# First block of a two-layer transformer kernel: the second group's rows loaded ahead of the FFN weights, bias and FFN statistics by tiles, FFN rows normalised on ScalarE, softmax sums ahead of the pieces' additions

## Chip, core and metric

The kernel runs on one core of one Trainium2 chip. The metric is the device time of one execution in microseconds (us). Three timed runs of the kernel before gave 2656.91, 2652.33 and 2652.30; the median is 2652.33. Engines are written as in the profile: PE is TensorE (matmuls), PEld its weight loads, DVE VectorE, ACT ScalarE, POOL GpSimd, SP SyncE, from whose queue all DMAs are issued. All data are float32.

## What is computed

The reference takes x of 2 sequences x 2048 tokens x 256 features through four sublayers; only the first is touched by the change. Cut to it:

```python
x = L0_attn_x                                   # (2, 2048, 256)
x = x + _L0_attn_ref(_layernorm(x), ...)        # first block
# within _L0_attn_ref(x, ...):
h = _layernorm(x, g1, b1)
q, k, v = h @ Wq + bq, h @ Wk + bk, h @ Wv + bv # 16 heads of 16, 4 key heads
q, k = _rope(q), _rope(k)
scores = q k^T / 4, masked to a window of 64    # each token sees itself and 63 before it
out = softmax(scores) @ v
x = x + (out @ Wo + bo)
h2 = _layernorm(x, g2, b2)
return x + gelu(h2 @ Wf1 + bf1) @ Wf2 + bf2     # FFN, 1024 wide
```

After it come a local attention block with an FFN (two layers), a gated block over the whole sequence, and a product with ternary weights.

## The kernel before

The 4096 tokens are 32 tiles of 128 (a tile: tokens on the 128 partitions), in 8 groups of four. The first block works tile by tile in steps. The table `steps` (lines 635 to 661) says which stage of which tile or group stands in which step: tile t is projected and taken (rope) in step t, its scores, masks and maxima stand in step t + 1, its transposed weights and values in t + 2, its output projection in t + 3. The first seven tiles (RAMP = 7) are projected a step early, as no FFN work fills their steps. For group g the first-layernorm statistics stand in step 4g - 3, its normalisation and transposes in 4g - 2, together with the residual rows y (`residual`, line 307), and the bias bo is added to y in step 4g + 1, four tiles at once. When a group's last tile is done, in step s = 4g + 7, the FFN of the group begins: `FfnA.statistics` over its four tiles and `FfnA.normalise`; its eight hidden products and four output products ("pieces") fill the next four steps in two places each, fill(0) and fill(1), and in step s + 5 the finished rows get their statistics and go, normalised, into R for the next block.

Inside a step, `step_a` (line 666) writes out the order by hand. PE, ACT, DVE and POOL each run their instructions strictly in that order (`manual_schedule`, line 1446); only the DMA queue of SP is ordered by the compiler's own scheduler. So what stands first in the text holds up whatever stands behind it on the same engine. Semaphores order the engines among each other.

Lines that the prediction speaks of:

- DMA: line 56 issues every load. Line 318 to 347 load the weights; the group's rows are loaded by `GroupA.__init__` (line 294), the values of a tile are copied to a shifted place by lines 431 and 433 (`vown` to `vmid`), and FFN weights of the next block are loaded in the step that projects tile 4 (line 673).
- First layernorm: L145 and L146 (DVE, statistics of one tile), L158, L159, L162 (POOL, power -1/2), L169 (rows normalised on DVE) or L176 and L178 (the same on ACT), L224 (PE transposes of a group), L229 (ACT takes them with gain and shift), L188 and L193 (residual rows y on ACT), L216 (POOL, four row additions, of the bias and of others).
- Tile: L402 (PE projection), L411, L425 (DVE), L417, L420, L428 (POOL), L438, L443 (DVE), L449, L450 (PE transposes), L455, L456, L458 (ACT copies), L468 (PE scores), L478 (DVE masks), L487 (DVE maxima), L488 (POOL subtracts them), L491 (ACT exponents), L522 (PE transposes of weights), L530 (ACT copies), L542 and L550 (PE values and sums), L560, L561 (DVE), L566 (PE output), L572 (DVE adds it to y). From tile 6 on the sums of the weights come from DVE instead of PE: L498 (sums), L501 (reciprocal), L508 (ACT spreads), L513 (PE transposes), L515 (ACT copies).
- FFN: L604 (PE hidden), L610 (ACT gelu), L615 (PE output), L622 (DVE addition), L135, L137 (POOL, power), L207 (rows normalised on DVE), L625 (stores the finished rows).
- Next block, in the change of block: L973 (PE projection), L985 (ACT), L994, L997 (POOL), L1029 (PE transposes), L1048 (PE scores).

The region allocator (`Region`, line 93) places the tiles of this block by tag in one large buffer, `room`; a tag with one buffer is written again only when its last reader is through.

Of the kernel before, what the change touches and what calls it, by code (L numbers as in the profile page):

```python
# [17 lines left out]
P = 128  # L18
# [27 lines left out]
def kernel(ctx: ExitStack, tc: tile.TileContext, I: dict, out: bass.AP):  # L46
# [241 lines left out]
    class GroupA:  # L288


        def __init__(self, g):
            self.g = g
            self.xg = T(wa, [P, GT, D], "xg", 1)
            load(self.xg, x_v[:, g * GT : (g + 1) * GT, :])
# [15 lines left out]

        def add_bias(self):
            add_rows(self.y, lambda t: boA)

# [15 lines left out]
    ropeA = T(wA, [P, TPS, 2, AHD], "ropeA")  # L329
    load(ropeA, I["rope_a"])  # L330

    woA = T(wA, [P, KC, D], "woA")
# [56 lines left out]
    class TileA:  # L389
# [94 lines left out]
        def maxima(self, half):  # L484
            Sh = self.S[:, half * 2 * AG : (half + 1) * 2 * AG, :]
            mc = T(small, [P, 2 * AG], "mxA")
            nc.vector.reduce_max(mc, Sh, axis=AX.X)  # L487
            nc.gpsimd.tensor_sub(Sh, Sh, mc.unsqueeze(2).to_broadcast([P, 2 * AG, P]))  # L488

        def exponents(self):  # L490
            nc.scalar.activation(self.S, self.S, AF.Exp, scale=1.0 / AHD**0.5)  # L491

# [81 lines left out]
    class FfnA:  # L574


        def __init__(self, grp):
            self.g, self.y = grp.g, grp.y
            self.xr = T(wa, [P, GT, D], f"xr{self.g % 2}", 1)
            load(self.xr, x_v[:, self.g * GT : (self.g + 1) * GT, :])  # L580

        def statistics(self):
            self.stats = statistics(self.y)

        def normalise(self):
            self.h = T(wa, [P, GT, D], "h", 1)
            if self.g == 0:
                mv, rs = self.stats
                normalised_on_scalar(self.y, mv[:, :, 0], rs, self.h)
            else:  # L590
                normalised(self.y, self.stats, self.h)
            add_rows(self.y, lambda t: bf2)

            add_rows(self.xr, lambda t: self.y[:, t, :])
# [28 lines left out]

        def last_statistics(self):
            nc.sync.dma_start(out=xs[:, self.g * GT : (self.g + 1) * GT, :], in_=self.xr)  # L625
            self.stats = statistics(self.xr)

# [19 lines left out]
    for g in range(NG):  # L647
        at(GT * g - 5, "load", g)
        at(GT * g - 3, "statistics", g)
        at(GT * g - 2, "normalise", g)  # L650
        at(GT * g + 1, "bias", g)
        s = GT * (g + 1) + 3
        at(s - 1, "residual", g)
        at(s, "prepare", g)

        if g < NG - 1:
            for c in range(ADFF // P):
                at(s + 1 + c // 4, f"fill{c // 2 % 2}", g, "hidden", c)
            for tt in range(GT):
                at(s + 3 + tt // 2, f"fill{tt % 2}", g, "output", tt)  # L660
        at(s + 5, "finish", g)

    groups_a, tiles_a, ffns_a = {0: first_group}, {}, {}
    steps_a = steps

    def step_a(todo):
        p = a = q = o = n = m = f = e = None
        for (g,) in todo.get("load", ()):
            if g:
                groups_a[g] = GroupA(g)  # L670
# [10 lines left out]
        if "output" in todo:  # L681
            o = tiles_a.pop(todo["output"][0][0])
        for (g,) in todo.get("residual", ()):
            ffns_a[g] = FfnA(groups_a[g])
        if "statistics" in todo:
            n = groups_a[todo["statistics"][0][0]]
        if "normalise" in todo:
            m = groups_a[todo["normalise"][0][0]]
        if "prepare" in todo:
            f = ffns_a[todo["prepare"][0][0]]  # L690
        if "finish" in todo:
# [15 lines left out]
        for (t,) in todo.get("project", ()):  # L707
            tiles_a[t].project()
        if p and p.t < RAMP:
            p.take()  # L710
            if q:
                q.mask(0)
                q.mask(1)
            p.rotate()
            if q:
                q.maxima(0)
                q.mask(2)
        else:
            if q:
                q.mask(0)  # L720
                q.mask(1)
            if p:
                p.take()
            if q:
                q.mask(2)
            if p:
                p.rotate()
            if q:
                q.maxima(0)
# [4 lines left out]
        if a and not pieces:  # L734
            a.weights_to_keys()
            a.take_weights()
        for r in pieces:
            r()
        if n:
            n.statistics()  # L740
        if f:
            f.statistics()
        if e:
            e.last_statistics()
        if o and not o.by_features:
            o.spread_sums()
        if p:
# [5 lines left out]
        if a and pieces:  # L753
            a.weights_to_keys()
            a.take_weights()
        for r in fill(1):
            r()
        if m:
            m.normalise()
        if f:  # L760
            f.normalise()
        if e:
# [10 lines left out]
        if m:  # L773
            m.to_features()
            m.residual()
        if f:
            f.to_features()
        if a and not a.by_features:
            a.sum_weights()
        for (g,) in todo.get("bias", ()):  # L780
            groups_a[g].add_bias()

# [1013 lines left out]
```

## Time and profile before

| what | us |
|---|---|
| median of three timed runs | 2652.33 |
| profiled execution, its own time | 2654.86 |
| its span, first to last instruction | 2653.1 |
| PE busy / DVE busy / ACT busy / POOL busy | 2569.6 / 1620.1 / 1221.2 / 993.9 |
| 0 to 15, PE busy and granted clock | 5.70 at 1.00 |
| 15 to 30 | 8.66 at 0.94 |
| 30 to 45 | 7.15 at 0.50 |
| 45 to 60 | 14.04 at 0.99 |
| 60 to 121 | 49.58 at 0.92 |
| 183 to 244 (one group of the steady part) | PE 59.00, DVE 50.46, ACT 36.20, POOL 34.96 |
| 491 to 552 (change to the next block) | 51.30 at 0.94 |

How to read it: the times in the profile are those of one execution, from its first instruction. A row of the timeline has the start, the duration, the engine, the line of the kernel, the operation, what it writes and reads, how many such instructions are merged, and in brackets how long the engine stood idle ahead of it and what ended that. Matmuls overlap, and their ends are modelled, so PE's busy time is no measure of its peak; holes between its rows are. The granted clock is the share of full speed at which TensorE was clocked.

### The profile page before, as it was taken

The numbers are of one execution on the slowest core, as the hardware profiler recorded it, in microseconds if no ns is written. First come the engines' busy times: TensorE is split into PE (matmuls) and PEld (weight loads), VectorE is DVE, ScalarE is ACT, GpSimd is POOL, SyncE is SP. The second block draws the span as 40 slices with busy tenths as digits, with TensorE's granted clock in tenths as the row PEclk, the third lists the DMA queues.
The fourth block names the chain that finished last, engine by engine and source line by source line (L and its number), as shares of the span: only waits on it lengthen the run. The fifth ranks groups of instructions, "written<-read, shape, count | busy, mean of one in ns | idle before, by whom it ended". The sixth has DMA issues, their size and how long they took to land.

```text
span 2653.1 us, 50755 instructions
## 1 busy us (share of the span) xinstructions
PE 2569.6 (97%) x19766; PEld 1638.2 (62%) x19766; DVE 1620.1 (61%) x4403; ACT 1221.2 (46%) x2567; POOL 993.9 (37%) x1237
## 2 busy tenths in 40 slices
PE   6899999898999999999999999999999999999998
PEld 4566666566667666666666676666544445445567
DVE  5778877557666776657666677774433435434344
ACT  3565655465666666656566666663510001500000
POOL 5555554445444444444544544541200002300011
PEclk8999999998999999999999999999999999999999
DMA  5010111111001101010311111101100000100000
GB/s 170 17 31 30 33 31 39 47 33 48 21 21 25 29 25 26 21 59 21 97 29 25 29 33 37 25 17 58 40 8 4 7 6 12 44 0 7 4 10 12
DMA packets 73167, 81.99 MB, mean 31 GB/s; under 512 B 18829, under 2 KB 57056, under 8 KB 72672
## 3 DMA queue, kind: packets, MB, share of 16 engines
q1 hardware_dynamic: 72928, 78.75, 10.7%
q8 instruction: 157, 2.57, 0.4%
q14 instruction: 82, 0.67, 0.1%
HBM read 44.20 MB, written 10.50 MB: 21 GB/s over the span
## 4 chain that ended last, share of the span: by engine, by line
PE 82%; DVE 9%; POOL 4%; issue 3%; DMA 1%; ACT 1%; SPq 1%; POOLq 0%; ACTq 0%; DVEq 0%
PE ps L1649 16%; PE ps L973 12%; PE ps L1227 10%; PE ps L1250 6%; PE ps L1573 4%; PE ps L1155 4%; PE ps L1048 3%; PE ps L1126 2%; PE ps L604 2%; PE ps L1592 2%; PE ps L1561 2%; PE ps L1098 2%; PE ps L1029 2%; PE ps L1551 2%; PE ps L615 2%
## 5 line engine op out<-in xcount | busy, mean ns | idle before, releaser
L1649 PE MATMUL ps<-room 128*128 128x512 f32 (+1 forms) x1152 | 463.2, 544 | 0.0
L1649 PEld LDWEIGHTS ps<-room 128*128 128x128 f32 x1152 | 217.8, 189 | 221.9 <-issue 214.7
L973 PE MATMUL ps<-room 128*128 128x512 f32 x768 | 347.2, 601 | 0.0
L1079 ACT ACTIVATE room<-room,shift,rn 128x192 f32<-128x192 f32 x512 | 276.0, 546 | 72.9 <-DVE shift L1067 72.9
L994 POOL TENSOR_TENSOR room<-room 128x256 f32<-128x256 f32 x128 | 112.9, 882 | 500.5 <-ACT room L985 500.5
L1227 PE MATMUL ps<-room 128*128 128x512 f32 x640 | 287.6, 593 | 0.4 <-ACT room L229 0.4
L1617 ACT COPY room<-ps 128x256 f32<-128x256 f32 x32 | 11.8, 370 | 587.9 <-PE ps L1615 587.9
L1012 POOL TENSOR_TENSOR rn<-ss,mhalf 128x8 f32<-128x8 f32 x128 | 248.5, 1941 | 10.7
L973 PEld LDWEIGHTS ps<-room 128*128 128x128 f32 x768 | 141.0, 190 | 157.7 <-issue 150.2
L1579 DVE SCALAR_TENSOR_TENSOR room<-ps,room 128x512 f32<-128x512 f32 (+1 forms) x144 | 90.1, 626 | 206.5 <-PE ps L1573 206.5
L1227 PEld LDWEIGHTS ps<-room 128*128 128x128 f32 x640 | 118.8, 190 | 137.3 <-issue 131.8
L1602 POOL TENSOR_SCALAR veC<-mvC 128x1 f32<-128x1 f32 x32 | 7.2, 224 | 453.1 <-DVE mvC L1600 453.1
L1250 PE MATMUL ps<-room 128*128 128x256 f32 x768 | 173.0, 379 | 0.0
L1060 DVE CUSTOM_DVE_ANT_0 room<-ps,room 128x192 f32<-128x192 f32 x512 | 152.2, 353 | 15.0 <-PE ps L1048 14.2
L1250 PEld LDWEIGHTS ps<-room 128*128 128x128 f32 x768 | 143.7, 190 | 24.8 <-issue 6.5
L1090 DVE TENSOR_SCALAR room<-room,rdB 128x192 f32<-128x192 f32 x512 | 151.7, 360 | 4.5
L1243 DVE SCALAR_TENSOR_TENSOR room<-ps,room 128x512 f32<-128x512 f32 x96 | 72.1, 751 | 125.8 <-PE ps L1227 87.0
L488 POOL TENSOR_TENSOR room<-room,mxA 128x1024 f32<-128x1024 f32 x64 | 120.3, 1896 | 58.8 <-DVE mxA L487 33.3
L1009 DVE TENSOR_REDUCE ss<-room 128x8 f32<-128x512 f32 x128 | 81.9, 681 | 94.3 <-ACT room L987 94.3
L1573 PE MATMUL ps<-room 128*128 128x512 f32 (+1 forms) x288 | 133.4, 545 | 0.0
L1155 PE MATMUL ps<-room 128*128 128x256 f32 x512 | 120.9, 379 | 0.0
L1155 PEld LDWEIGHTS ps<-room 128*128 128x128 f32 x512 | 97.3, 190 | 34.1 <-issue 23.2
(190 smaller groups left out, 5032.7 us busy)
## 6 DMA issues: line engine op xcount, KB each, us to landing
room<-room SPq DMA_DIRECT2D x144, 128.0 KB
room<-in_L_attn_x_dram SPq DMA_DIRECT2D x16, 512.0 KB
room<-in_rope_b_dram SPq DMA_DIRECT2D x16, 512.0 KB
xs<-room SPq DMA_DIRECT2D x8, 512.0 KB
room<-xs SPq DMA_DIRECT2D x8, 512.0 KB
room<-in_rope_c_dram SPq DMA_DIRECT2D x8, 512.0 KB
out_dram<-R SPq DMA_DIRECT2D x32, 128.0 KB
room<-in_L_ffn_w_dram SPq DMA_DIRECT2D x6, 640.0 KB
```

The lines of the kernel that those rows point to most:

```text
L488: nc.gpsimd.tensor_sub(Sh, Sh, mc.unsqueeze(2).to_broadcast([P, 2 * AG, P]))
L973: nc.tensor.matmul(pm, src[:, cols], self.w["wqkv"][:, k, part * BIN : (part + 1) * BIN], start=k == 0, stop=k == 1,)
L994: nc.gpsimd.tensor_mul(u2[:, :, 0:hd2], x[:, :, hd2:BHD], sin[:, :, 0:hd2].to_broadcast([P, BH, hd2]))
L1012: nc.gpsimd.tensor_tensor(self.rn[part], ss, mhalf[:, 0:BH], ALU.pow)
L1060: nc.vector.tensor_tensor_reduce(S[:, e, jj, :], sc[e][:, jj * KW : (jj + 1) * KW], self.mask[:, jj, :], 1.0, -3.0e38, ALU.add, ALU.max, t ...
L1079: nc.scalar.activation(S[:, e, jj, :], S[:, e, jj, :], AF.Exp, bias=self.shift[half][:, a : a + 1], scale=self.rn[0][:, head : head + 1], ...
L1090: nc.vector.tensor_scalar_mul(S[:, e, jj, :], S[:, e, jj, :], rd[:, a : a + 1])
L1155: nc.tensor.matmul(pm[:, 0:D], self.oT[:, k, :], wo[:, k, :], start=k == 0, stop=k == BIN // P - 1)
L1227: nc.tensor.matmul(pm, w["w1"][:, k, half, c * P : (c + 1) * P], hT[:, k, :], start=k == 0, stop=k == KC - 1,)
L1250: nc.tensor.matmul(pm[:, 0:D], hh[:, c, tt * P : (tt + 1) * P], self.w["w2"][:, c, :], start=c == 0, stop=c == BNC - 1,)
L1573: nc.tensor.matmul(pm[:, 0:n], self.KT[:, J * P : (J + 1) * P], self.QT[:, q0 : q0 + n], start=True, stop=True,)
L1649: nc.tensor.matmul(acc[e][:, 0:n], self.V[:, J, e * P : (e + 1) * P], s2, start=J == 0, stop=J == TPS - 1,)
```

## The change

- The second group's rows are loaded right behind the rope table, ahead of Wo and the FFN weights (`second_group = GroupA(1)`), into the place `xr1`, since `xg` holds the first group. Its statistics stand in step 0 instead of 1, its normalisation and transposes in step 1 instead of 2, its residual rows in step 3 instead of 2.
- The bias is added to y one tile a step (steps 4g + 1 to 4g + 4) instead of four tiles in step 4g + 1.
- The FFN's statistics are taken one tile a step, each after the tile's output is added; the last at the very start of step s. The finished rows' statistics are split in two steps of two tiles.
- The FFN rows are normalised on ACT in all groups (before: group 0 alone), right behind the copies of the weights (L530), and the additions on POOL follow where the whole stood before.
- The sums of the weights (L498, L501) stand ahead of the additions of fill(1), and their spreading (L508) ahead of fill(0)'s gelus or additions; before, both stood behind them.
- In the first seven tiles the exponents are two instructions of half a tile each.
- The maxima lie in the region (two buffers) instead of the small pool (three).

No arithmetic is added or left out.

```diff
-            self.xg = T(wa, [P, GT, D], "xg", 1)
+            self.xg = T(wa, [P, GT, D], "xr1" if g == 1 else "xg", 1)
...
-        def add_bias(self):
-            add_rows(self.y, lambda t: boA)
+        def add_bias(self, i):
+            nc.gpsimd.tensor_add(self.y[:, i, :], self.y[:, i, :], boA)
...
     load(ropeA, I["rope_a"])
+    second_group = GroupA(1)
...
-            mc = T(small, [P, 2 * AG], "mxA")
+            mc = T(wa, [P, 2 * AG], "mxA")
...
-            nc.scalar.activation(self.S, self.S, AF.Exp, scale=1.0 / AHD**0.5)
+            for S in (self.S[:, 0 : 2 * AG, :], self.S[:, 2 * AG :, :]) if self.t < RAMP else (self.S,):
+                nc.scalar.activation(S, S, AF.Exp, scale=1.0 / AHD**0.5)
...
-        def statistics(self):
-            self.stats = statistics(self.y)
+        def statistics(self, i):
+            st = T(small, [P, 6], "st")
+            nc.vector.bn_stats(st, self.y[:, i, :])
+            nc.vector.bn_aggr(self.mv[:, i, :], st)
+            if i == GT - 1:
+                self.rs = rstd_of(self.mv)
...
             self.h = T(wa, [P, GT, D], "h", 1)
-            if self.g == 0:
-                mv, rs = self.stats
-                normalised_on_scalar(self.y, mv[:, :, 0], rs, self.h)
-            else:
-                normalised(self.y, self.stats, self.h)
+            normalised_on_scalar(self.y, self.mv[:, :, 0], self.rs, self.h)
+
+        def residual(self):
             add_rows(self.y, lambda t: bf2)
...
-        at(GT * g - 3, "statistics", g)
-        at(GT * g - 2, "normalise", g)
-        at(GT * g + 1, "bias", g)
+        early = 1 if g == 1 else 0
+        at(GT * g - 3 - early, "statistics", g)
+        at(GT * g - 2 - early, "normalise", g)
+        at(GT * g - 2 + early, "residual", g)
         s = GT * (g + 1) + 3
-        at(s - 1, "residual", g)
-        at(s, "prepare", g)
+        for i in range(GT):
+            at(GT * g + 1 + i, "bias", g, i)
+
+            at(GT * g + 4 + i, "row_statistics", g, i)
+        at(s - 1, "begin", g)
+        at(s + 4, "last_statistics", g)
...
         for (t,) in todo.get("project", ()):
             tiles_a[t].project()
+        for g, i in todo.get("row_statistics", ()):
+            if i == 0:
+                ffns_a[g] = FfnA(groups_a[g])
+            if i == GT - 1:
+                f = ffns_a[g]
+                f.statistics(i)
...
         if a and not pieces:
             a.weights_to_keys()
             a.take_weights()
+            if f:
+                f.normalise()
+        if o and not o.by_features:
+            o.spread_sums()
         for r in pieces:
             r()
         if n:
             n.statistics()
-        if f:
-            f.statistics()
+        for g, i in todo.get("row_statistics", ()):
+            if i < GT - 1:
+                ffns_a[g].statistics(i)
+        for (g,) in todo.get("last_statistics", ()):
+            ffns_a[g].last_statistics((0, 1))
         if e:
-            e.last_statistics()
-        if o and not o.by_features:
-            o.spread_sums()
+            e.last_statistics((2, 3))
...
         if a and pieces:
             a.weights_to_keys()
             a.take_weights()
+        if f and not (a and not pieces):
+            f.normalise()
+        if a and not a.by_features:
+            a.sum_weights()
         for r in fill(1):
             r()
         if m:
             m.normalise()
         if f:
-            f.normalise()
+            f.residual()
...
         if m:
             m.to_features()
-            m.residual()
+        if y:
+            y.residual()
         if f:
             f.to_features()
-        if a and not a.by_features:
-            a.sum_weights()
-        for (g,) in todo.get("bias", ()):
-            groups_a[g].add_bias()
+        for g, i in todo.get("bias", ()):
+            groups_a[g].add_bias(i)
```

## Prediction

> **What bounds the kernel now.** I read the page first, then who waited for whom on PE, then PE's idle time stretch by stretch, and last the timeline of the stretches where PE idles. The page's busy times (PE, PEld, DVE, ACT, POOL) and its PEclk row:
>
> ```profile
> PE 2569.6 (97%) x19766; PEld 1638.2 (62%) x19766; DVE 1620.1 (61%) x4403; ACT 1221.2 (46%) x2567; POOL 993.9 (37%) x1237
> PEclk8999999998999999999999999999999999999999
> ```
>
> PE is the bound nearly everywhere; what can be won is the time in which it idles. All edits lie in the first block (0 to about 550 us); the later blocks only shift. Adding up the holes between PE's rows there gives, per 61.5 us: 15.1, 11.4, 1.9, 1.9, 1.8, 1.9, 1.9, 2.9, 9.6 us. So there are three stretches: a ramp (0 to 110 us), a steady part (period 61.5 us, four steps of one tile), and the change of block (480 to 550). Who ended PE's waits (us in all, times, longest):
>
> ```profile
> PE ps L449 <- DVE room L443: 15.2, 9, 7.8
> PE ps L224 <- DVE room L169: 9.7, 2, 9.3
> PE ps L513 <- ACT room L508: 5.2, 7, 1.5
> PE ps L449 <- DVE room L438: 4.3, 9, 1.2
> PE ps L224 <- ACT room L178: 4.2, 4, 3.8
> PE ps L224 <- DVE room L207: 4.2, 9, 1.1
> ```
>
> The ramp's timeline (start, duration, then in brackets the idle time ahead and what ended it):
>
> ```profile
> 16.88 0.21 DVE L443 TENSOR_TENSOR room<-room 128x64 f32<-128x64 f32 x1
> 25.30 0.38 SPq L56 DMA_DIRECT2D room<-in_L_attn_x_dram  x1
> 31.91 0.43 DVE L145 BATCH_NORM_STATS2 st<-room 128x6 f32<-128x256 f32 x1 [6.78 <-DMA room<-in_L_attn_x_dram]
> 40.76 1.09 PE L449 MATMUL ps<-ident,room 128*128 128x128 f32 x4 [7.85 <-DVE room L443]
> ...
> 102.71 0.33 PE L224 MATMUL ps<-ident,room 128*128 128x128 f32 x1 [3.75 <-ACT room L178]
> 105.44 2.01 PE L468 MATMUL ps<-room 32*64 32x128 f32 x64
> ```
>
> DVE, which takes its work in order, stands 6.78 us for the second group's rows, issued only at 25.30; behind it wait tile 2's projection and PE (7.85 us). At 102.71 PE waits for the first FFN rows; afterwards the granted clock is 0.50 (105 to 110 us) and 64 score matmuls take 2.01 us instead of 1.21. The steady part:
>
> ```profile
> 351.89 0.77 PE L224 MATMUL ps<-ident,room 128*128 128x128 f32 x5 [0.38 <-DVE room L207]
> 359.79 0.44 PE L513 MATMUL ps<-ident,room 128*128 128x128 f32 x2 [0.53 <-ACT room L508]
> ...
> 374.07 0.63 PE L449 MATMUL ps<-ident,room 128*128 128x128 f32 x4 [0.54 <-DVE room L443]
> ...
> 382.89 2.33 DVE L498 TENSOR_REDUCE room<-room 128x8 f32<-128x1024 f32 x2
> 385.43 1.22 DVE L478 TENSOR_TENSOR room<-ps,room 128x512 f32<-128x512 f32 x2
> 389.02 0.66 PE L449 MATMUL ps<-ident,room 128*128 128x128 f32 x4 [0.43 <-DVE room L438]
> ```
>
> These four holes make 1.87 us a group. Two of them come from L498 and L501, which run 382.89 to 385.4 after L572 and push the masks L478 past the end of the scores (PE L468, 383.65).
>
> **Ramp, part by part.** Times after the change are worked from the rows of before.
> (1) *Second group's rows early.* The load goes ahead of Wo, at 7.52 (where the first Wo load was issued). The first x load landed 4.4 us after issue, the second 6.6, so 12 to 14 us; DVE reaches the statistics at 17.0. Each DMA behind it is issued some 0.5 us later; the first of these that are needed (vown copies, for L542 at 35.6) were issued from 25.78 with the x load ahead of them, so they hardly move.
> (2) *Statistics in step 0.* 2.41 us on DVE (31.91 to 34.32) from 17.0, so tile 1's L411 moves from 17.01 to 19.4; POOL's L162 (2.0) then holds L417, and the second maximum L487 ends at 27.05 (before 25.1).
> (3) *Normalise in step 1.* L178 (2.08) stands ahead of the exponents on ACT: 27.2 to 29.3; two half exponents end at 31.5, at 1.1 each: no row shows one, it lies between 0.52 (128x256) and 1.91 (128x2048), and the line between these gives 1.1; the ends would move the chain by under 1.6 in this step alone. PE's L224 x8 stand ahead of the scores L468, which run 30.0 to 31.2; DVE's masks wait for them (3 us). Transposes L522 of tile 0 run 32.7 to 34.6, L530, L542 and L550 end at 35.6, 36.6, 37.6, and DVE's reciprocal L560 starts at 37.65 (before 45.55): **7.9 us ahead**.
> (4) *Step 3.* DVE alone: L411 of tile 3 at 39.75, L560 of tile 1 at 46.05 (before it waited 1.51 for PE), L411 of tile 4 at 48.7 (before 58.05): **9.4 ahead**. L488 and the bias of one tile (0.70 of L216's 2.76 for four) lie beside DVE.
> (5) *Steps 4 and 5.* A row statistic (0.53: L145 and L146) is added to each step of a DVE that never waits: L411 of tile 6 at 69.5 (before 77.82): **8.3 ahead**.
> (6) *Step 6.* Four bias adds on POOL (3.04, from 77.51) shrink to one, so L417 and L420 no longer hold L438: it comes 2.35 after L411 (0.58 + 0.49 + 1.27 of DVE's own) instead of 4.07. Gain 1.7, less 2 x 0.53 of statistics: **8.9 ahead** at step 7's first mask.
> (7) *Step 7.* Before, L487 ended at 98.25, then came 2.2 of statistics and 1.3 of POOL before L178 at 102.05. Now L178 starts at 89.5, 0.2 after L487. L224 ends at 92.2. L455 to L458 now follow L178 on ACT, so L468 runs 92.6 to 93.8, L402 to 95.3 (2.86 becomes 1.56 at full clock, as PE's 3.75 us hole is gone), and L229 releases the last of the first L604 pair at 96.25: **14.4 ahead**. POOL's eight L216 and one bias now run just before L417, which ends the next L449's wait 0.6 late: **13.8 ahead** when the steady part begins.
>
> **Steady part.** Work per group is the same on PE; on DVE less by L207 (2.21), on ACT more by 2.08, both with room (50.4 and 36.3 busy in 61.5). Sums L498 run while PE does the second fill, where DVE waited 2.8 us (382.55, 395.52). Masks then start when L468 ends; L443 ends some 5.2 us into the step and PE needs it at 6.1 (L468, L402, fill: 1.14 + 1.49 + 3.44): the 0.54 and 0.43 go. Spreading the sums (L508) ahead of L610 takes the 0.53; rows normalised on ACT at 347 to 349 are ready for L224 at 350.8: the 0.38 goes. The exponents fall 1.2 us later (347.80 to 349), and the transposes that need them stand at 360. POOL's eight adds start after L488 (347.8) and end with the bias at 354, ahead of L417 at 356.4. The finishing statistics (L145, L146) only move, two of four to the step before. The maxima get two buffers of the room instead of three of a small pool: one is written again a tile (15 us) after its reader L488, so nothing; if it did wait, L487 would stand under 2 us in a DVE with 11 idle. Six groups of 1.87: **11.2 us**. Bounds: 0, if other waits take the holes, to 11.2, as PE has no others there. I take 11.2, as each cover is 0.9 us or more.
>
> **Change of block.** L513 waited 1.07 and 1.46 for L508 behind L610: gone. L224 waited 1.08 + 0.40 + 0.40 for L207: the last tile's statistics come before the last FFN output, L178 runs 516 to 518, gone. POOL's adds end 2.7 earlier against 1.9 of PE: 0.8. Sum **5.2 us**.
>
> **Sum.** 13.8 + 11.2 + 5.2 = 30.2. The profiled execution took 2654.86 (span 2653.1); it lies 2.5 above the median of the runs, 2652.33. Forecast 2652.3 - 30.2 = **2622.1**.
>
> **Two rules weighed.** L425 (two SBUF inputs) took 0.87 at 78.40 beside POOL's L216 and 0.49 elsewhere. The Trainium skill (SBUF — State Buffer, Who interferes with whom) has such a VectorE operation contend with a GpSimd one that reads SBUF; by it a bias beside each of four ramp tiles' L425 costs 4 x 0.38 = 1.5, and the sum would be 28.7. That sentence speaks against the bias by tiles; I leave it out, since by (4) the bias falls beside L560, which reads PSUM. Second, after holes of 2.09 and 1.59 us (526 to 531) the clock was 0.50 and L1048 took 3.57 instead of 1.57, L973 6.02 instead of 5.35. The Trainium skill (TensorE: Matmul & The Clock Gate, Part 1) halves the clock after an idle window of about 3.4 us; the trace agrees only if two short holes count together. My holes there stay (1.8 and 1.6), so the cost stays; the other outcome is rival C.
>
> **Rivals.**
> A. *The steady holes come back elsewhere* (ACT, with four more activations a group, or POOL late). For it: those waits are short, and several units finish close together. Against: the room above. 30.2 - 11.2 = 19: 2633.
> B. *The ramp loses a third*. FFN weight loads wait for POOL's L256, which moves from 46.24 to 48.75, behind the bias; then tile 3's vown copies, 6.5 us behind it, are issued at 55.3 for L542 at 62, with 4.4 to 6.6 us to land. Or DVE's steps stretch. Price 5: 2627.
> C. *The clock survives the change of block*: 2.0 + 0.67 more: 2619.4.
> D. *No change*: statistics by tiles (0.53 a step) and the early L178 and L224 hold up the ramp as much as the load frees it, and A too, so that only 5.2 are left: 2647, just inside 0.2%.
> E. *Slower*: the vown copies of B. The trace lists no landing of theirs. Each us past 62 holds L542, and with it all engines; it turns to a loss when they land over 30 us late, after 92. At 40 us late: 2662. Against: some 4.8 MB of loads at the 239 GB/s of 45 to 60 us take 20 us in all.
>
> **Chances.** Forecast 0.58, A 0.17, B 0.12, C 0.05, D 0.04, E 0.04. So faster by over 0.2% (5.3 us, about what a measurement of this kernel tells from no change) 0.92, same 0.04, slower 0.04. The range 2614 to 2637 reaches from C less 5 to A plus 4, for errors in the ramp's chain of sums, and leaves out D and E.
>
> **What would show it.** The second x load at 7.5 and L145 following L443 with no DMA wait; PE's first wait for L449 of tile 2 under 3 us; the first L604 near 96; a period of 59.6; no waits on L207 and L508 in PE's list; tile 8's L417 near 98. Wrong would be: a DMA wait on L542; L449 waits still at 0.4 or more in the steady part; L224 waiting for L178.

## The result, and the profile after it

The changed kernel took 2616.22 us (median of 4 runs, 2614.68 to 2618.3), the kernel before 2654.62 in the runs beside it (median of 4). The ratio is 0.9855, 95% interval 0.9838 to 0.9872: 38.4 us faster, where 30.2 were forecast. The profiled execution after took 2614.68 (span 2612.8); against the span before it is 40.3 shorter.

In the kernel after, most lines of the first block stand a few lines lower: L411, L417, L425, L443, L449, L468, L478 and L487 are now L413, L419, L427, L445, L451, L470, L480 and L489; L402 is L404, L550 is L554; L488 and L491 are L490 and L495; L498 is L502, L508 L512, L513 L517, L522 L526, L560 L564, L561 L565, L604 L613, L615 L624, L1029 L1064.

The page's busy times and clock row, after:

```profile
PE 2557.2 (98%) x19766; PEld 1637.9 (63%) x19766; DVE 1612.8 (62%) x4382; ACT 1233.4 (47%) x2602; POOL 993.1 (38%) x1237
PEclk9999999998999999999999999999999999999999
```

PE's busy time fell by 12.4 us, although it computes the same; what that means is said below. Who ended PE's waits, after (us in all, times, longest):

```profile
PE ps L451 <- DVE room L445: 6.0, 7, 1.8
PE ps L224 <- ACT room L178: 4.4, 5, 3.6
PE ps L526 <- DVE room L565: 3.4, 1, 3.4
```

The waits on L207 and L508 are gone, those on L443 (now L445) fell from 15.2 to 6.0; one on L565 is new. The ramp's timeline after:

```profile
16.54 0.41 DVE L145 BATCH_NORM_STATS2 st<-room 128x6 f32<-128x256 f32 x1
...
26.30 1.90 POOL L490 TENSOR_TENSOR room<-room 128x1024 f32<-128x1024 f32 x1 [0.55 <-DVE sh L176]
26.80 1.75 DVE L427 TENSOR_TENSOR room<-room 128x320 f32<-128x320 f32 x1
27.03 2.80 PE L224 MATMUL ps<-ident,room 128*128 128x128 f32 x8 [3.64 <-ACT room L178]
29.76 2.01 PE L470 MATMUL ps<-room 32*64 32x128 f32 x64
...
39.06 1.76 DVE L564 RECIPROCAL room<-ps 128x256 f32<-128x256 f32 x1 [1.89 <-PE ps L554]
...
71.03 2.06 PE L526 MATMUL ps<-ident,room 128*128 128x128 f32 x12 [3.38 <-DVE room L565]
...
93.94 1.21 PE L470 MATMUL ps<-room 32*64 32x128 f32 x64
```

The second group's statistics run at 16.54 with no wait ahead of them; the first value sums are taken at 39.06 (45.55 before), the first FFN matmuls L613 start at 96.55 (110.08 before), and the L451 behind them at 101.05 (113.51 before). The steady part is read best from start to start: the step is the distance from one tile's scores (L468, after L470) to the next one's. Four steps of one group took 14.82, 15.03, 15.93 and 15.72 us before (from 290 to 353), 61.50 in all; after, 14.08, 14.08, 14.99 and 14.99, **58.13** in all. From 101 us on the kernel after has no row of PE's waits until the change of block (488).

| where | before | after | ahead | forecast |
|---|---|---|---|---|
| tile 8's scores, behind the first FFN pieces | 121.41 | 108.97 | 12.4 | 13.8 |
| last scores of the first block | 475.52 | 442.82 | 32.7 | 25.0 |
| first L1029 (after: L1064) | 528.66 | 490.20 | 38.5 | 30.2 |
| end of the span | 2653.1 | 2612.8 | 40.3 | 30.2 |

So the ramp gave 12.4 (13.8 forecast), the steady part 20.3 (11.2), the change of block 5.8 (5.2). The last 1.8 us arise in the later blocks and were not followed.

### The profile page after: what moved, and what is told of

It reads as the page before. It is cut to its first block, busy times and chain, and to the rows that moved or that the text cites. A ratio compares the mean times of both kernels' runs of the same rounds, so it can differ in the third digit from the quotient of the medians.

```text
span 2612.8 us, 50767 instructions
## 1 busy us (share of the span) xinstructions
PE 2557.2 (98%) x19766; PEld 1637.9 (63%) x19766; DVE 1612.8 (62%) x4382; ACT 1233.4 (47%) x2602; POOL 993.1 (38%) x1237
## 3 DMA queue, kind: packets, MB, share of 16 engines
q1 hardware_dynamic: 72928, 78.75, 10.6%
## 4 chain that ended last, share of the span: by engine, by line
PE 92%; DVE 4%; POOL 3%; issue 1%; DMA 0%; ACT 0%; POOLq 0%; ACTq 0%; DVEq 0%; SPq 0%
PE ps L1684 17%; PE ps L1008 12%; PE ps L1262 11%; PE ps L1285 6%; PE ps L1608 4%; PE ps L624 4%; PE ps L1190 4%; PE ps L613 4%; PE ps L1083 3%; PE ps L1161 2%; PE ps L1627 2%; PE ps L1596 2%; PE ps L1133 2%; PE ps L1064 2%; PE ps L1586 2%; PE ps L526 2%
## 5 line engine op out<-in xcount | busy, mean ns | idle before, releaser
L1029 POOL TENSOR_TENSOR room<-room 128x256 f32<-128x256 f32 x128 | 114.1, 891 | 500.8 <-ACT room L1020 500.8
L1652 ACT COPY room<-ps 128x256 f32<-128x256 f32 x32 | 11.8, 370 | 587.7 <-PE ps L1650 587.7
L490 POOL TENSOR_TENSOR room<-room 128x1024 f32<-128x1024 f32 x64 | 120.3, 1896 | 60.3 <-DVE room L489 44.1
```

The costliest lines, as they stand in the source:

```text
L1029: nc.gpsimd.tensor_mul(u2[:, :, 0:hd2], x[:, :, hd2:BHD], sin[:, :, 0:hd2].to_broadcast([P, BH, hd2]))
```

## The experiments

Theory after the result: three edits act in three places, and the steady part gave more than forecast because PE's waits there cost more than the idle time drawn ahead of them. Rival: one edit (the rows that leave VectorE) makes the room, and the order of the sums is incidental. The first four runs take the edits apart. Steps are quoted as above, from scores to scores. A gain over before is counted against the runs of before on the same chip; a distance to after is one of medians.

**Second group early, alone.**

```diff
+            self.xg = T(wa, [P, GT, D], "xr1" if g == 1 else "xg", 1)
...
+    second_group = GroupA(1)
...
+        early = 1 if g == 1 else 0
+        at(GT * g - 3 - early, "statistics", g)
+        at(GT * g - 2 - early, "normalise", g)
+        at(GT * g - 2 + early, "take_rows", g)
```

> The kernel before with the second group's edit alone: its rows loaded ahead of Wo, its statistics and normalisation one step earlier, its residual rows where they were. Theory (the three edits add up, each where it acts): only the ramp moves. Without the row statistics (0.53 a step) that the whole change adds there, step 7's first mask L478 comes 8 to 10 us earlier than 91.33, the first L604 as much ahead of 110.08, the steady period stays at 61.5 us, and the gain is 8 to 10 us. Rival (the ramp moves only together with the early FFN rows, because DVE is full there): under 3 us. Rival (the phase of the steady part matters): the period moves too, and the gain is over 12.

Measured 2648.07, 7.8 us faster (ratio 0.9968, 0.9955 to 0.9981). The scores of tile 7, at 105.44 before, start at 97.89, 7.5 ahead; the period stays at 61.5. The mechanism of the theory holds, the gain lies just below its 8 to 10; of the ramp and the steady part, the edit acts in the ramp alone. (The group's residual rows are not where they were, as the expectation says, but one step later, as in the change.)

**Order of the sums, alone.**

```diff
+        if o and not o.by_features:
+            o.spread_sums()
         for r in pieces:
             r()
...
+        if a and not a.by_features:
+            a.sum_weights()
         for r in fill(1):
             r()
```

> The kernel before with the order of the sums alone: spreading the sums (L508) goes ahead of the pieces' additions and gelus, and the sums themselves (L498, L501) ahead of the second fill's. Theory (PE's waits for L443, L438 and L508 cost more than the idle time drawn ahead of them: from start to start 0.68, 0.70 and 0.60 us rather than 0.52, 0.54 and 0.43, and the last mask L478, which frees a PSUM bank, holds the transposes L522 by 0.13 to 0.29 more in three of four steps): the period falls from 61.5 to 58.7, six times 2.8 make 17, the change of block gives 2.5 to 3, together 19 to 20 us. The prediction's own terms: six times 1.5 and 2.5, 11.5 us. Rival (the rows that leave DVE make the room, the order alone does little): under 6 us, and L449 still waits 0.4 or more.

Measured 2644.18, 11.7 us faster (0.9953, 0.9938 to 0.9968), not 19 to 20. Three of the four steps did fall to 14.08, 14.08 and 14.99, as after; but the fourth *grew* from 15.72 to 16.69, so that the period is 59.83. This timeline of the run shows the fourth step:

```profile
340.67 2.33 DVE L498 TENSOR_REDUCE room<-room 128x8 f32<-128x1024 f32 x2
...
343.49 2.19 DVE L207 TENSOR_SCALAR room<-room,mv,rs 128x256 f32<-128x256 f32 x4
...
345.00 0.33 PE L224 MATMUL ps<-ident,room 128*128 128x128 f32 x1 [0.41 <-DVE room L207]
```

The sums now stand ahead of the FFN rows' normalisation L207 in VectorE's queue, and PE's transposes L224 wait for it. A wait has taken the place of those removed, and what would remove it is the *other* edit. That the gain, 11.7, is near the 11.5 which the expectation worked out from the prediction's own terms is chance: three steps gave more than the idle time drawn in them, and the fourth took 0.97 back.

**FFN rows, row statistics and bias by tiles, alone.** The core of the edit; bias by tiles, the last statistics, the half exponents and the place of the maxima are as in the change.

```diff
-            if self.g == 0:
-                mv, rs = self.stats
-                normalised_on_scalar(self.y, mv[:, :, 0], rs, self.h)
-            else:
-                normalised(self.y, self.stats, self.h)
+            normalised_on_scalar(self.y, self.mv[:, :, 0], self.rs, self.h)
...
+            at(GT * g + 4 + i, "row_statistics", g, i)
...
+        if f and not (a and not pieces):
+            f.normalise()
         for r in fill(1):
             r()
```

> The kernel before with the FFN part alone: row statistics by tiles, FFN rows normalised on ScalarE ahead of the second fill, bias by tiles, the last statistics two and two, half exponents in the ramp. Theory: in the steady part only the wait for the FFN rows goes (0.60 from start to start), period 60.9; the ramp gains 4 to 6 in step 7, where L178 no longer waits for the statistics behind the second maximum; the change of block 2 to 3; together 10 to 13 us. Rival (DVE, freed of 2.2 us of L207 a group, also masks earlier, and the sums' order adds little): the period falls to 59.5 or less and the gain is 18 or more.

Measured 2645.59, 10.3 us faster (0.9962, 0.9948 to 0.9977). The scores of tile 7 start at 100.13, 5.3 ahead; the period is 61.43, only 0.07 less. The rival is out: a VectorE with 2.2 us less to do per group changes nothing by itself. The theory's 0.60 did not come either: in the fourth step the wait of 0.38 for L207 went and one of 0.25 for the rotation (L443; L444 in this run) came, because the sums at the end of the step still push the masks and the rotation, and the edit itself adds the last tile's row statistics between the two:

```profile
332.57 0.37 DVE L590 BATCH_NORM_STATS2 st<-room 128x6 f32<-128x256 f32 x1
...
333.08 1.25 DVE L479 TENSOR_TENSOR room<-ps,room 128x512 f32<-128x512 f32 x2
...
336.78 0.63 PE L450 MATMUL ps<-ident,room 128*128 128x128 f32 x4 [0.25 <-DVE room L444]
```

The masks start 2.70 us behind the scores (330.38), in the same step before 2.18 (336.87 to 339.05). That is the prediction's rival A, at one hole.

**The change without the sums' order.** The two edits of the second run taken back in the kernel after.

> The kernel after with the sums put back where they were (L508's spreading behind the pieces, the sums L498 and L501 at the end of the step); all else as after. Theory: period 60.9 instead of 58.1, and 18 to 20 us of the 38 are lost, so 2634 to 2637. By the prediction's own terms 11.5 are lost (2628). Rival (the freed DVE does it): under 6 us are lost and L449's waits stay under 0.2.

Measured 2638.64, 17.2 us faster than before (0.9937, 0.9922 to 0.9952), so 21 of the 38 us are lost (22.4 by the medians), a little more than the theory's 18 to 20; the period is 61.43, not 60.9, for the reason just given. The order of the sums is worth 11.7 us alone and 21 with the other edits in place. The table of the steady part:

| | period | PE's waits listed from 115 us to the block's last scores, us in all |
|---|---|---|
| before | 61.50 | 11.1 |
| sums alone | 59.83 | 4.8 |
| rows alone | 61.43 | 10.6 |
| both (after) | 58.13 | none |

**Which half of the rows' edit is it: the engine, or the place in the queue?** Two runs. First the order of the sums with the rows on ScalarE at their old place, behind the second fill:

```diff
-            if self.g == 0:
-                mv, rs = self.stats
-                normalised_on_scalar(self.y, mv[:, :, 0], rs, self.h)
-            else:
-                normalised(self.y, self.stats, self.h)
+            mv, rs = self.stats
+            normalised_on_scalar(self.y, mv[:, :, 0], rs, self.h)
```

> The kernel before with the order of the sums, and the FFN rows of all groups normalised on ScalarE, but at their old place behind the second fill. In the run with the sums alone three of the four steps fell to 14.08, 14.08 and 14.99 us, and the fourth grew from 15.73 to 16.69, where L224 waits for L207, now queued on DVE behind the sums L498. Theory (the place in DVE's queue makes that wait, not the engine: L176, which gives ScalarE its shifts, stands behind the sums too): the fourth step stays at 16.2 to 16.7, period 59.3 to 59.8, gain over before 11 to 14 us. Rival (it is the 2.2 us of L207 on DVE): the fourth step falls to 14.99, period 58.1, gain 18 to 22.

Measured 2644.73, 9.4 us faster (0.9959, 0.9944 to 0.9974), 2 us less than expected; the fourth step is 16.77 and the period 59.9, as the theory has it, just above its 16.7 and 59.8. The run's timeline:

```profile
344.05 0.15 DVE L176 SCALAR_TENSOR_TENSOR sh<-mv,rs 128x4 f32<-128x4 f32 x1
...
344.23 2.07 ACT L178 ACTIVATE room<-room,sh,rs 128x256 f32<-128x256 f32 x4 [4.17 <-DVE sh L176]
```

ScalarE stood idle for 4.17 us, for an operation of 0.15 us that was queued on VectorE behind the sums (L498, from 341.23). Then the reverse, the kernel after with the rows on VectorE, at their new place:

```diff
-            normalised_on_scalar(self.y, self.mv[:, :, 0], self.rs, self.h)
+            if self.g == 0:
+                normalised_on_scalar(self.y, self.mv[:, :, 0], self.rs, self.h)
+            else:
+                normalised(self.y, (self.mv, self.rs), self.h)
```

> The kernel after with the FFN rows of every group but the first normalised on VectorE (L207 in place of L178), at their new place ahead of the sums. Theory (the place counts): L207 runs at once behind the row statistics, L224 finds its rows, the sums come 2.2 us later but still ahead of what needs them; period 58.1 to 58.4 and 0 to 2 us over after. Rival (the engine counts): L224 or the next L449 waits, period 59.5 or more, 8 us or more over after.

Measured 2615.37 (0.9851, 0.9834 to 0.9867), no different from after; period 58.23. The engine is worth 0.1 us a group; the place, together with the row statistics by tiles, which no run took apart from it here, 1.6 and more. VectorE and PE of this run in the fourth step:

```profile
322.32 2.38 DVE L207 TENSOR_SCALAR room<-room,mvF,rs 128x256 f32<-128x256 f32 x4
...
324.62 2.33 DVE L502 TENSOR_REDUCE room<-room 128x8 f32<-128x1024 f32 x2
...
326.45 1.04 PE L224 MATMUL ps<-ident,room 128*128 128x128 f32 x8
```

The rows are ready 1.7 us ahead of L224, and the sums behind them are still in time. The row statistics by tiles have their part in this: with the sums alone, all four ran in this step (338.23 to 340.4), and POOL had the factors ready only at 341.9, behind the start of the sums (340.67).

**The load's place.** The kernel after with the second group's load behind the first block's weights.

```diff
-    second_group = GroupA(1)
...
     load(bf2, bcast_rows(I["L0_attn_bf2"], D))
+    second_group = GroupA(1)
```

> The kernel after with the load of the second group's rows issued behind the weights again, where before had it; statistics and normalisation stay one step earlier. Theory (the load's place is what lets the statistics come early; DVE takes its work in order): L145 waits until about 32, as before, and now tile 1's L411 with everything behind it stands too, so that 11 to 15 us are lost against after: 2627 to 2631, at or above what before gives with the other two edits. Rival (the rows land early anyway once nothing waits on the queue): under 3 us lost.

Measured 2622.46 (0.9878, 0.9863 to 0.9893), 6.2 slower than after: neither of the two. The edit was less than the expectation took it for: behind the weights, but ahead of the small scale loads that stood before it in the kernel before, the load was issued at 18.01, not 25.30. The run's VectorE:

```profile
23.39 0.43 DVE L145 BATCH_NORM_STATS2 st<-room 128x6 f32<-128x256 f32 x1 [7.20 <-DMA room<-in_L_attn_x_dram]
```

It starts 6.85 later than after's 16.54, and tile 1's scores come at 36.63 in place of 29.76, 6.87 later. The block's last scores are 7.04 later. The mechanism is the theory's: each us that the rows are late, with VectorE waiting in order, is about a us of the ramp; only the lateness was less than expected.

**Half exponents.** Back to one operation of 1.91 us in the ramp.

```diff
-            for S in (self.S[:, 0 : 2 * AG, :], self.S[:, 2 * AG :, :]) if self.t < RAMP else (self.S,):
+            for S in (self.S,):
```

> The kernel after with the exponents of the ramp's tiles in one operation of 1.91 us again instead of two of 1.06 (the first of which can start a maximum earlier). Theory (in the ramp DVE sets the pace from 39 us on, so a chain that ends 0.85 earlier on ScalarE is worth something only in the first steps): 0 to 1.5 us slower than after. Rival (each ramp step's chain counts): 0.85 in each of six steps, 4 to 5 us slower.

Measured 2615.99 (0.9856, 0.9839 to 0.9872): no difference. PE does wait for the exponents then (up to 2.42, behind 67.25), and not for L565 (3.38 becomes 0.51): in a stretch where VectorE sets the pace, one wait takes the place of another.

**What is left in the ramp.** Three runs and a fourth that mended the third. In the kernel after, VectorE is idle only once from 57 to 93 us (0.29, at 87.25), and PE's largest wait behind the first rows, 3.64 at 27.03, is for L178, whose shifts L176 stand behind both maxima. First, the third group's rows on ScalarE, to take L169 (3.13 us there) off VectorE:

```diff
-            if self.g == 1:
+            if self.g in (1, 2):
```

> The kernel after with the third group's rows (group 2) normalised on ScalarE as the second's are. Theory: in the ramp DVE runs without a gap from 55 to 93 us of the run after, so what leaves it is gained: its four L169 there took 3.13 us at 77.92, beside POOL's L490, while ScalarE had room; 1.5 to 3 us faster than after. Rival (PE's L224 then waits for ScalarE, whose rows come 0.52 us apart, and ScalarE's exponents come later): no change or 1 us slower.

Measured 2616.26 (0.9854, 0.9839 to 0.9868): no difference; the rival was right, for a reason that it did not name:

```profile
76.99 1.90 POOL L490 TENSOR_TENSOR room<-room 128x1024 f32<-128x1024 f32 x1 [0.55 <-DVE room L489]
...
77.29 1.61 DVE L176 SCALAR_TENSOR_TENSOR sh<-mv,rs 128x4 f32<-128x4 f32 x1
...
78.99 2.07 ACT L178 ACTIVATE room<-room,sh,rs 128x256 f32<-128x256 f32 x4 [3.68 <-POOL room L490]
```

L176, 0.15 us elsewhere, ends at 78.90, when POOL's L490 ends (78.89), and ScalarE stood idle meanwhile. So the next run moved such shifts ahead of the maxima: at first the second group's alone, rows included.

```diff
             p.rotate()
+            if m and m.g in (1,):
+                m.shift()
+            if m and m.g == 1:
+                m.normalise()
             if q:
                 q.maxima(0)
```

> The kernel after with the second group's normalisation earlier within its step: the shifts L176 and ScalarE's L178 stand right behind the rotation L445, ahead of the first maximum L489, in place of behind the second. Theory (in the run after, PE stands 3.64 us at 23.39 for L178, which waits for L176 behind both maxima, and is cold afterwards; the masks L480 at 31.83 wait 3.29 for its scores L470): rows at 22.7 to 24.8, L224 follows L452 with little wait, L470 near 26, masks near 28.5 behind L427; 2.5 to 4 us gained, 2612 to 2614. Rival (DVE, full from 39 us on, is delayed by something else in the same step, POOL's L490 or the exponents): under 1 us.

Measured 2613.07 (0.9845, 0.983 to 0.986), 3.1 faster than after by the medians; the two intervals overlap, so the traces decide. PE's wait of 3.64 is gone, tile 1's scores come at 26.07 in place of 29.76, and at the block's last scores it is still 3.65 us ahead (439.17, after 442.82). Then all three:

```diff
-            if m and m.g in (1,):
+            if m and m.g in (1, 2):
                 m.shift()
...
             if p:
                 p.rotate()
+            if f and f.g == 0:
+                f.shift()
```

> As the run before this one, and more of the same kind: the third group's rows normalised on ScalarE (as in the run that did only this) but with their shifts L176 ahead of the maxima, so that they do not meet POOL's L490; and the first FFN rows' shifts ahead of the maxima of step 7. Theory (a 0.15 us operation on DVE queued behind 2.4 us of maxima and held for 1.61 by L490 is what made ScalarE and PE late): besides the 2.5 to 4 of the first part, 1.5 to 3 at step 6 (L169's 3.13 leave DVE) and about 1.5 at step 7 (L224 from 92.4 instead of 93.9); in all 5.5 to 8 us faster than after, 2608 to 2611. Rival (the exponents, now behind L178 on ScalarE, or PE's order take it back): 2 to 4 us only.

Measured 2611.57 (0.9837, 0.9822 to 0.9852), 4.6 faster than after, between the rival's 2 to 4 and the theory's 5.5 to 8. Tile 7's scores, ahead of the first FFN pieces, start at 85.70 (93.94 after), 8.2 ahead, and the next step takes 18.42 in place of 15.03. The run's PE and POOL:

```profile
86.30 5.78 POOL L220 TENSOR_TENSOR room<-room 128x256 f32<-128x256 f32 x8
...
94.53 0.63 PE L459 MATMUL ps<-ident,room 128*128 128x128 f32 x4 [2.67 <-DVE room L453]
95.10 2.96 PE L534 MATMUL ps<-ident,room 128*128 128x128 f32 x16
```

POOL's eight residual additions (L216 in after, L220 here) had been hidden; with all else earlier they and the bias behind them hold the rotation's products on POOL (L427 in this run, L419 in after) until 92.93, PE's L459 waits, and its cold rows behind that take longer: L534 2.96, otherwise 1.91, and the eight L625 behind it 4.27, otherwise 3.62. The last run puts them one step later:

```diff
-            f.residual()
+            if f.g == 0:
+                late.append(f)
+            else:
+                f.residual()
...
             q.maxima(1)
+        while late:
+            late.pop().residual()
```

> The kernel of the run a_early with POOL's eight residual additions L220 of the first group (5.8 us) one step later, behind the second maximum's subtraction. In a_early the seventh step's scores came 8.2 us earlier than after's, but the next step took 18.42 in place of 15.03: POOL stood in L220 from 86.30 and then in the bias L321, so that the rotation L427 and PE's L459 came 2.67 late, and the cold PE took 2.96 for L534 and 4.27 for a piece. Theory (POOL's queue ahead of the rotation is what took the gain back): that step takes 15.0 to 15.3, and 3 us are won over a_early, 2608 to 2609. Rival (those additions hold the rotation of the step after as much, or something else is late at the first pieces): no gain over a_early's 2611.6.

Measured **2607.54** (0.9821, 0.9807 to 0.9834), 48.1 faster than before and, by the medians, 8.7 faster than after. The step takes 13.89, less than expected, and tile 8's scores, at 108.97 in after, come at 100.16. In that step PE's L459 comes at 92.26 with no wait, L534 takes 1.91 again, and POOL's L220 runs from 96.55, behind the rotation. This is the fastest version of the study; its interval does not meet that of after (0.9838 to 0.9872).

## Why the prediction was right, and where it was off

The three places and the waits in them were the right ones, and 2616.22 lies in the stated range, 2614 to 2637. It lies there with some luck: the steady part gave 9.1 more than forecast, which the range did not provide for. Its lower end was set by rival C less 5, and C did not come; the room kept for it, and the 1.4 that the ramp fell short, took up the excess. (The kernel before also measured 2.3 us higher beside it than the median from which the forecast counts.)

**Ramp: 13.8 forecast, 12.4 measured.** The load at 7.5 (7.59), statistics that follow L445 with no DMA wait (16.54), the first L604 near 96 (96.55): each came nearly as written. Tile 8's L417 came at 99.45, not near 98. Most of the error was made in part (3), and stayed: 7.9 ahead was forecast at the first L560, 6.5 were measured, and the next milestones are off by as much (at tile 6's L411 8.3 forecast, 6.7 measured; at step 7's first mask 8.9 and 7.2). That part has the scores at 30.0 to 31.2, at full clock; they began in time, at 29.76, but took 2.01, and L404 behind them 2.81 instead of 1.56: together 2.05 us longer, at a granted clock of 0.50 (24 to 34 us). The prediction counts such cold rows in step 7 and left them out here. In step 7 it was right: PE has no long wait there, and the half clock is gone (L470 1.21). Part (4) to (6) were sums of a VectorE that never waits; they hold, as the later milestones show. Part (6), four bias additions that shrink to one on POOL, has L438 2.35 behind L411 in place of 4.07; measured 2.18 (L440 at 73.32, L413 at 71.14).

That L224 waits for L178 was listed as a sign of error. The 3.64 at 27.03 lies within the prediction's own sum, L178 from 27.2 with PE behind it; in step 7 the wait is down from 3.75 to 0.28.

**Steady part: 11.2 forecast, 20.3 measured.** This is the term that was mis-sized: "six groups of 1.87". The holes it names were the right ones, and all of them went. But 1.87 is the idle time *drawn* ahead of PE's rows, and a group lost 3.37. From tile 8's scores to the block's last, PE was busy for 342.19 of 354.11 us before and for all of 333.85 after: 11.9 of the 20.3 were idle time, near the 11.2 forecast, and 8.3 were counted as busy. The difference is seen from start to start. PE's timeline before:

```profile
308.44 3.60 PE L604 MATMUL ps<-room 128*128 128x512 f32 x8
312.58 0.63 PE L449 MATMUL ps<-ident,room 128*128 128x128 f32 x4 [0.54 <-DVE room L443]
...
328.34 2.20 PE L522 MATMUL ps<-ident,room 128*128 128x128 f32 x16
328.65 0.67 DVE L478 TENSOR_TENSOR room<-ps,room 128x512 f32<-128x512 f32 x1
...
329.44 0.85 PEld L522 LDWEIGHTS ps<-ident,room 128*128 128x128 f32 x8 [0.31 <-issue]
```

and the same places after:

```profile
285.90 3.60 PE L613 MATMUL ps<-room 128*128 128x512 f32 x8
289.34 0.60 PE L451 MATMUL ps<-ident,room 128*128 128x128 f32 x4
...
304.09 1.78 PEld L526 LDWEIGHTS ps<-ident,room 128*128 128x128 f32 x16
...
304.20 1.91 PE L526 MATMUL ps<-ident,room 128*128 128x128 f32 x16
```

First, the eight FFN matmuls hold PE for 3.44 us from their start to L451's when nothing is waited for, though their row is drawn as 3.60: the modelled end overlaps the next row by 0.16. Before, the distance was 4.14, so the wait was 0.70, of which 0.54 are drawn. At the four holes of a group this hides 0.16, 0.16, 0.17 and 0.22, in all 0.71. Second, the transposes L522 took 2.03 from their start to the next row's before (328.34 to 330.37, L615) and 1.74 after (304.20 to 305.94, L624), and no wait is listed at all. The row of the weight loads shows it: before, they come as eight and eight, the second eight 0.31 late, at 329.44, right behind the end of the last mask L478 (329.32); after, sixteen in a row. It is so in all four steps: where the last mask ends late (314.30, 329.32 and 344.44), the second eight start 0.11 to 0.12 behind it, and in the first step, where it ends at 298.52, before the transposes start, the loads are in one row. So it is the last mask that they wait for; that the reason is the PSUM bank which the mask reads is inferred, and was not tried by itself. In three steps of four this is 0.20, 0.29 and 0.14. Together 1.87 + 0.71 + 0.63 = 3.21 of 3.37. The hidden 1.34 of it, six times, 8.0, is the larger part of the 12.4 us by which PE's *busy* time fell: some of what the page counts as PE at work was PE waiting.

The prediction gave 11.2 as the upper bound, "as PE has no others there". That sentence was wrong: PE had waits that its rows do not show.

**Why no other wait took the holes.** Rival A was given 0.17, and the single runs show how near it was: with the sums alone the fourth step grew by 0.97, with the rows alone the saving of one hole came back as another, and only both together reach 58.13. The prediction summed the holes as if each belonged to one edit. In the ramp that holds well enough (7.5 and 5.3 ahead alone, 11.8 together, without the sums); in the steady part it does not: 1.67 and 0.07 us a group alone, 3.37 together.

**Change of block: 5.2 forecast, 5.8 measured.** The holes of 2.09 and 1.59 stayed, as forecast (2.17 and 1.59 at 490.20 and 492.45), and the half clock behind them too (0.50 from 492 to 498 us); rival C did not come. B did not come either: PE waits for no DMA. D and E are far off. That the 5.2 came out does not show its three terms one by one: the waits for L508 and L207 are gone, the 0.8 of POOL's additions was not followed.

**Two small edits that did nothing.** The half exponents (0) and ScalarE as the engine for the later groups' rows (0.1 us a group): the prediction gave the first no gain of its own, and let the 0.38 a group go by the engine and the earlier place together, where the place did it. The bias by tiles, the split of the last statistics and the place of the maxima were not run alone.

## What to carry to other kernels

Size a wait from start to start, against the same rows where nothing is waited for, and not by the idle time drawn ahead of a row: here 1.87 us a group were drawn and 3.37 were there to be had; a row of weight loads that breaks in two showed a wait that PE's list of waits has not. Moving work ahead in one engine's queue moves it ahead of something: look at what is now behind it, and take edits to the same queue as one edit, since alone they gave 1.67 and 0.07 us and together 3.37. A small operation that another engine needs (a shift of 0.15 us) belongs ahead of the long ones in its queue; in the ramp that was worth 3.1 us, with its like 8.7 once POOL's hidden additions had been moved too.

## What the runs showed of the hardware

**VectorE held by POOL.** Three kinds of VectorE operations that read SBUF alone were held up to the end of POOL's L490 (1.90 us, SBUF): in the kernel after L427 took 1.75 in place of 0.49, ending 0.35 behind the end of L490 (26.30 to 28.20), and four L169 took 3.13, otherwise 1.37 (the first was held to the end of L490, the second to that of the bias L313 behind it); in the run with the third group on ScalarE, L176 took 1.61 in place of 0.15, ending when L490 did. The maximum L489 (1.22), which reads SBUF too, did not stretch beside L490, nor did the masks L480, which read PSUM. The Trainium skill (SBUF — State Buffer, Who interferes with whom) has just these kinds: two SBUF inputs, or a tensor_scalar in its two-port mode, shut out by a GpSimd instruction until that ends, and reductions free of it; the traces agree, with 1.61 for an operation of 0.15 (in which mode L169 ran they do not show). The prediction had weighed that rule for L425 beside L216, where it saw 0.38, and not beside the longer L490.

**The clock and short waits.** A single wait of 2.67 us was enough for the half clock. Windows of PE in the run with all three shifts early (columns: stretch, length, then busy time of PE, PEld, DVE, ACT and POOL with counts, then the granted clock, the DMA share and GB/s):

```profile
91.00:94.00 3.00, 0.86 (x3) 0.03 (x1) 0.05 (x1) 0.69 (x1) 3.00 (x7) 1.00 0.00 0
...
96.00:97.00 1.00, 1.00 (x6) 1.00 (x5) 0.96 (x2) 1.00 (x3) 1.00 (x1) 0.50 0.14 33
```

PE was busy for 0.86 of the three us from 91 to 94, and for some 3.4 us from 95.8 on it had half the clock. And in the run where the wait of 3.64 had gone, the clock still fell to 0.50 from 24 to 30 us, behind a stretch (20 to 23) in which PE was busy for 1.15 of 3 us with no wait over 1.85. The Trainium skill (TensorE: Matmul & The Clock Gate, Part 1) names an idle window of about 3.4 us for this. The traces differ: here shorter holes were enough, one of 2.67 us or two with work between them. Whether the window is shorter or need not be idle throughout, no run here tells.
